# The second column group of the first batch's keys, formed by one whole unit behind the first scores

## The chip, the cores and the metric

The kernel runs on one core of a Trainium2 chip. The metric is the device time of one execution in microseconds. Every time below comes from the runs of the kernel before the change, or from one profiled execution of it. In the profile the engines are called PE (TensorE matmul), PEld (TensorE weight load), DVE (VectorE), ACT (ScalarE), POOL (GpSimd) and SP (the engine that only issues transfers). A name such as L410 is line 410 of the kernel before.

## The reference, cut to what matters

The reference is one block of a Perceiver: a cross-attention of 128 query rows to 2048 context rows for each of 8 batches, then a causal self-attention, then a feed-forward layer with quantised numbers. Only the cross-attention's beginning is touched.

```python
q = (layernorm(x) @ Wq)          # x: 8 batches x 128 rows x 512
k = context @ Wk                 # context: 8 x 2048 x 384
v = context @ Wv
sim = einsum('bihd,bjhd->bhij', q, k) * SCALE     # 8 heads of 64
out = softmax(sim) @ v
x = x + out @ Wo + bo
# then x = x + self_attention(layernorm(x)), and x = x + feed_forward(layernorm(x))
```

All is computed in 32-bit floating point. TensorE runs such a product as two matmul instructions, so the profile shows two MATMUL rows for each product of the program.

## The kernel before, in words

**Keys and values.** The context is handed over transposed, with 384 rows (three blocks of 128) and 2048 columns. A batch has two halves of 1024 columns, `x_{b}_0` and `x_{b}_1`. The projections to keys and to values are cut into 4 x 3 x 2 blocks, and the usual 24 block products are replaced by 20 (`block_product`), which need sums of blocks: 20 additions over a half of the context (`sum_half`, L168) and 13 additions with 4 copies over the weights (`sum_w`, copies at L185, additions L189 to L202). A key unit (`k_proj`, L410) makes one of two column groups `f2` of the keys; its `halves` say for which context halves. With both halves it has 40 matmul calls with 256 columns, with one half 20. A value unit (`v_proj`, L433) makes the values of one half. The units write seven PSUM banks, which are read as soon as they are whole: by ScalarE copies (L329) and by VectorE additions (L332 and L335, one operand in PSUM; L367, both operands in SBUF). A later product into the same bank waits for that reading.

**The start.** The first half of the first batch's keys is made without sums, by `k_plain` (L392, copies at L399): for each column group 12 matmul calls with 512 columns. Beside them the queries are prepared in two groups of four batches. `q_norm` computes each row's statistics on VectorE (L454, L456), the root on ScalarE (L457) and the normed rows on VectorE (L458, L460). `q_turn` transposes them on TensorE (L94) with ScalarE copies (L95), and `q_proj` projects them (L477, copies L481) and stores the result to DRAM (L482), from where `load_q` brings each batch's part.

**The order around the change.** TensorE, ScalarE and VectorE keep the order in which the program is written. Before the change it is: weight sums for keys (VectorE), plain keys of group 0, norm of the first four rows, plain keys of group 1 up to a point in its second half, transposes of the first rows, norm of the last four rows, the rest of the plain keys, projections with the second transposes between them. Meanwhile VectorE forms the sums of both context halves and of the value weights, and then prepares the self-attention's weights: `dot` and `weight_by_bias` (L268), which multiply a weight by a row of biases, and `turn_weight` (L281), which transposes a weight in 32 x 32 blocks that are then moved by 16 transfers on SP (L285). On GpSimd, `bo` is loaded into a buffer that the first L268 row must have left (L847), and added to the eight query tiles (L486). Then come the key unit of group 0 for the second half only, the values of the first half (with the second L268 row and the second L281 row in its VectorE order), the first scores (L509, evacuated at L513), the key unit of group 1 for the second half only with the first exponentials (L533), the product of two self-attention weights (`both_weights`, L296), and the values of the second half. From there on the loop is regular. `next_half(b, h)` loads a context half of a later batch on SP (L129) and forms its sums on GpSimd (L168); it can begin once the half that had the buffer has been read for the last time. The strips of the turned probabilities (L552) are on SP too.

**The loads at the start.** The key weights come in six transfers on ScalarE's queue (L214), the first context half in six on SP (L222), then four query tiles (L232), the query weights, the last four query tiles (L235), the second context half, the value weights and the self-attention weights.

Of the kernel before, what the change touches and what calls it, by code (L numbers as in the profile page):

```python
# [9 lines left out]
F32 = mybir.dt.float32  # L10
# [10 lines left out]
P = 128  # L21
# [4 lines left out]
def tile_perceiver_block(  # L26
# [21 lines left out]
    nc = tc.nc  # L48
    B, S, D = x.shape
# [15 lines left out]
    GB = B // NG  # L65
# [22 lines left out]
    xs = {}  # L88
# [17 lines left out]
    pp, ptp, tmp, xp = right("pp", 1), right("ptp", 1), right("tmp", TMPB), right("xp", 2)  # L106
# [15 lines left out]
    def x_tiles(b, h):  # L122
        xraw[b, h] = ctxp.tile([P, NKC, 4, BK], F32, tag=f"x{h}", name=f"x_{b}_{h}")
        xmore[b, h] = ctxp.tile([P, 8, BK], F32, tag=f"m{h}", name=f"m_{b}_{h}")
# [84 lines left out]

    w_in = keep.tile([P, 2, NKC, D], F32, tag="keep", name="w_in")  # L210
    wk, wv = w_in[:, 0], w_in[:, 1]
    for f2 in range(2):
        for k in range(NKC):
            nc.scalar.dma_start(wk[:, k, ts(f2, 256)], xa_wk[ts(k, P), ts(f2, 256)])  # L214

    early = bank("early")
    for _ in range(EARLY):
        nc.tensor.matmul(early[:, :P], ident, ident, start=True, stop=True)
    x_tiles(0, 0)
    for n in range(2):  # L220
        for k in range(NKC):
            nc.sync.dma_start(  # L222
                xraw[0, 0][:, k, 2 * n : 2 * n + 2],
                ctx_t[0, ts(k, P), ts(n, 512)].rearrange("p (i j) -> p i j", i=2),
            )

    x_in = ptp.tile([P, B, D], F32, tag="pT", name="x_in")
    for b in range(B):
        xs[b] = x_in[:, b, :]
    xd = dram.tile([P, B, D], F32, tag="xd", name="xd")  # L230
    for b in range(GB):
        nc.sync.dma_start(xs[b], x[b])  # L232
    wq = load_w(wop, xa_wq, NK, "wq", nc.sync)
    for b in range(GB, B):
        nc.sync.dma_start(xs[b], x[b])  # L235
    load_half(0, 1)
# [69 lines left out]
    wv3 = wv.rearrange("p k (j n) -> p k j n", j=2)  # L306
    wk_sums = wxa.tile([P, len(WSLOT), 2, P], F32, tag="wk_sums", name="wk_sums")
    wv_sums = wxa.tile([P, len(WSLOT), 256], F32, tag="wv_sums", name="wv_sums")
    sum_w(lambda k, j: wk4[:, k, :, j, :], wk_sums, nc.vector)

    kts, vts, ps_, sums, qts, turned_, pos, nms, wides, mxs = [
        {} for _ in range(10)
    ]
# [70 lines left out]
    def k_plain(f2):  # L384


        k_tile(0, f2)
        for n in range(2):
            pss = [bank(f"k_{f2}_{j}_{n}") for j in range(2)]
            for k in range(NKC):  # L390
                for j in range(2):
                    nc.tensor.matmul(  # L392
                        pss[j], wk4[:, k, f2, j, :], xraw[0, 0][:, k, 2 * n : 2 * n + 2],
                        start=(k == 0), stop=(k == NKC - 1),
                    )
                if (n, k) == (1, 0):
                    yield
            for j in range(2):
                nc.scalar.copy(kts[0, f2][:, j, ts(n, 512)], pss[j])  # L399

# [390 lines left out]
    def all_of(unit):  # L791
        for _ in unit:
            pass

    def first_of(unit):
        next(unit)
        return unit

    def next_half(b, h):
        if b < B:  # L800
            load_half(b, h)
            sum_half(b, h, nc.gpsimd)
# [19 lines left out]
        sa0.bv, sa0.u, sa0.mask = w[2:]  # L822
        return sap, w, sa0

    all_of(k_plain(0))
    both = [q_norm(0)]
    rest = first_of(k_plain(1))
    qds = [q_turn(0, both[0])]
    both.append(q_norm(1))
    all_of(rest)  # L830
    q_proj(0, both[0], qds[0], range(2))
    qds.append(q_turn(1, both[1]))

# [21 lines left out]
    first_of(values)  # L855
    turn_weight(1)
    all_of(values)
    next_half(1, 0)

    wo = load_w(wop, xa_wo, NK, "wo", nc.sync, tag="wq")  # L860

# [35 lines left out]
    for b in range(B):  # L897
        last = b + 1 == B
        for m in range(NK):
            scores(b, m)  # L900

            if m % 2 and not last:
                after_strips(b, m)
            if m == 1 and b > 0 and not last:
                load_u(b - 1)
            if m == 3 and b > 0 and not last:
                nc.scalar.dma_start(xtd[:, :, ts(b - 1, S)], stats[b - 1])
                nc.scalar.dma_start(xr[:, b - 1, :], xs[b - 1])
            if m == 3 and b < B - 2:
                load_x(b)  # L910
            unit = None
            if m > 0:
                attend(b, m - 1)
            elif b > 0:

                attend(b - 1, NK - 1)
            if m == 0:
                unit = v_proj(b, 1)
            elif not last and m == 1:
                unit = v_proj(b + 1, 0)  # L920
            elif not last:
                unit = k_proj(b + 1, m - 2)
            elif m == 1:
                unit = sa0.keys(sa0.rows)
            elif m == 2:
                unit = sa0.weights_and_values(sa0.rows[:3])
            else:

                sa1 = SelfAttention(1, sap, w)
            if b == m == 0:  # L930

                keys = k_proj(0, 1, (1,))
                first_of(keys)
                first_of(keys)
                exps(b, m, 0)
                all_of(keys)
            else:
                exps(b, m, 0)
                if unit and not (last and m > 0):
                    first_of(unit)  # L940
            if m == 3 and last:
                bring_rows()
                for r in sa0.rows:
                    sa0.probabilities(r)
# [24 lines left out]
            if unit:  # L969
                all_of(unit)  # L970
            if m == 1 and b > 0 and not last:
                row_scale(b - 1)
            if m == 3:
                next_half(b + 2, 0)
            if m == 0:
                next_half(b + 1, 1)
                if not last:
                    load_q(b + 1)
                if b > 0:
                    project(b - 1, ot)  # L980
                if last:
                    sap, w, sa0 = enter_self_attention()
# [189 lines left out]
    for i, unit in enumerate(work):  # L1172
# [7 lines left out]
        if i > 2:  # L1180

            b = i - 3
# [63 lines left out]
```

## Time and profile before

| what | us |
|---|---|
| median of 3 runs (lowest, highest) | 1086.6 (1086.08, 1086.62) |
| the profiled execution's own time | 1086.99 |
| its span on the core | 1085.2 |
| TensorE busy with matmuls | 1079.3 |
| VectorE busy | 757.9 |
| ScalarE busy | 352.4 |
| GpSimd busy | 234.3 |

The stages at the beginning, in the chain of work that ended last (start in us): plain keys from 4.9, first transposes at 23.5, the remaining plain keys at 25.3, query projections at 28.7, half-unit of the keys at 57.9, values at 67.2, first scores at 84.4, product of weights at 98.3, values of the second half at 112.0, second scores at 129.3.

To read the lines that follow: a row of the timeline gives start, duration, engine, line, operation, what is written and read, and in brackets how long the engine had been idle and what ended that. A row of stretches gives for each engine its busy time in the stretch, then the clock granted to TensorE (1.00 is full), the busy share of the DMA engines and their rate. "Landing" is the time from the issue of a transfer to its last byte.

### The profile page before, as it was taken

Reading aid. Unit: us, or ns where it says so; the run is one execution under the profiler, and the core shown is the slowest. Engines: PE = TensorE matmul, PEld = TensorE weight load, DVE = VectorE, ACT = ScalarE, POOL = GpSimd, SP = SyncE. Lnnn points to the kernel's source line nnn. Section 1 sums busy time; section 2 is a strip of 40 time slices with the busy share of each in tenths; the row PEclk is TensorE's granted clock in tenths of the full one; section 3 lists DMA queues with packets and bytes.
Section 4 is the critical chain, followed back from the end, with each engine's and each line's share of the span. In section 5 each row is a group of like instructions: output and inputs, shape, how many; then the busy total and the mean of one; then the engine's idle time right before and its main releaser. Section 6 shows DMA issues by size and latency. Waiting matters only on the chain.

```text
span 1085.2 us, 16609 instructions
## 1 busy us (share of the span) xinstructions
PE 1079.3 (99%) x6198; PEld 816.0 (75%) x6198; DVE 757.9 (70%) x1639; ACT 352.4 (32%) x559; POOL 234.3 (22%) x350
## 2 busy tenths in 40 slices
PE   9999999999999999999999999999999999999998
PEld 5475788878887888787777878887888656768875
DVE  4876567778777877787778777777877657584233
ACT  3322233324332423432343234332433222323221
POOL 0144040351045005500550054025100212000000
PEclk9999999999999999999999999999999999999999
DMA  9476334553565456545544653555345644431001
GB/s 326 139 186 152 118 80 98 136 146 84 131 156 134 95 131 156 136 89 132 147 120 98 157 146 78 118 137 146 79 109 149 197 129 146 175 104 32 10 12 57
DMA packets 71855, 134.81 MB, mean 124 GB/s; under 512 B 28240, under 2 KB 36448, under 8 KB 70752
## 3 DMA queue, kind: packets, MB, share of 16 engines
q1 hardware_dynamic: 61120, 113.03, 40.7%
q0 software_dynamic: 3312, 11.03, 3.2%
q10 hardware_dynamic: 7344, 9.70, 2.9%
q8 instruction: 49, 0.80, 0.3%
q14 instruction: 30, 0.25, 0.1%
HBM read 54.01 MB, written 10.49 MB: 59 GB/s over the span
## 4 chain that ended last, share of the span: by engine, by line
PE 97%; SPq 1%; DMA 1%; DVE 1%; ACT 0%; issue 0%
PE pv_z L433 21%; PE pk_z L410 20%; PE po L564 11%; PE sc L509 10%; PE pv_b L433 4%; PE pk_b L410 3%; PE ph_b L1071 3%; PE psk L720 3%; PE psv L764 3%; PE pf L1119 3%; PE pq L477 3%; PE py L647 3%; PE ph_c L1071 2%; PE ph_a L1071 2%; PE k L392 2%; PE ph L1023 1%
## 5 line engine op out<-in xcount | busy, mean ns | idle before, releaser
L533 ACT ACTIVATE p<-p,nm 128x2048 f32<-128x2048 f32 x64 | 128.2, 2003 | 274.9 <-DVE nm L521 158.8
L546 DVE STREAM_TRANSPOSE p<-p 128x512 f32<-128x512 f32 x256 | 158.9, 679 | 63.1 <-ACT p L533 62.9
L513 DVE TENSOR_SCALAR_CACHE_REDUCE p<-sc 128x512 f32<-128x512 f32 x256 | 159.0, 686 | 20.9 <-PE sc L509 20.9
L168 POOL TENSOR_TENSOR m<-x 128x256 f32<-128x256 f32 x70 | 51.2, 732 | 495.5 <-DMA x<-in_ctx_t_dram 421.0
L433 PE MATMUL pv_z<-wv_sums,x 128*128 128x256 f32 x640 | 157.9, 381 | 0.0
L410 PE MATMUL pk_z<-x,wk_sums 128*128 128x256 f32 x600 | 150.0, 382 | 0.7 <-ACT kt L329 0.6
L433 PEld LDWEIGHTS pv_z<-wv_sums,x 128*128 128x128 f32 x640 | 120.6, 190 | 18.5 <-issue 2.2
L564 PEld LDWEIGHTS po<-pT,v 128*64 128x64 f32 x2048 | 111.1, 137 | 23.8 <-issue 22.3
L410 PEld LDWEIGHTS pk_z<-x,wk_sums 128*128 128x128 f32 x600 | 112.5, 190 | 20.3 <-issue 2.0
L564 PE MATMUL po<-pT,v 128*64 128x128 f32 x2048 | 118.9, 274 | 0.0
L509 PE MATMUL sc<-kt,q 64*128 64x512 f32 x512 | 118.5, 602 | 0.0
L433 PE MATMUL pv_z<-wv_sums,m 128*128 128x256 f32 x448 | 107.4, 380 | 0.0
L410 PE MATMUL pk_z<-m,wk_sums 128*128 128x256 f32 x420 | 101.4, 380 | 0.0
L433 PEld LDWEIGHTS pv_z<-wv_sums,m 128*128 128x128 f32 x448 | 83.4, 190 | 12.6 <-issue 0.8
L509 PEld LDWEIGHTS sc<-kt,q 64*128 64x128 f32 x512 | 46.9, 186 | 59.5 <-issue 54.6
L410 PEld LDWEIGHTS pk_z<-m,wk_sums 128*128 128x128 f32 x420 | 78.4, 190 | 11.7 <-DVE kt L332 0.4
L329 ACT COPY v<-pv_z 128x512 f32<-128x512 f32 x112 | 62.8, 589 | 55.8 <-PE pv_z L433 55.5
L329 ACT COPY kt<-pk_z 128x512 f32<-128x512 f32 (+1 forms) x112 | 59.8, 562 | 58.7 <-PE pk_z L410 58.2
L168 POOL TENSOR_TENSOR x<-x 128x256 f32<-128x256 f32 x98 | 69.9, 732 | 0.6 <-DMA x<-in_ctx_t_dram 0.6
L332 DVE TENSOR_TENSOR v<-pv_z,v 128x512 f32<-128x512 f32 x96 | 63.1, 685 | 5.5 <-PE pv_z L433 5.5
L332 DVE TENSOR_TENSOR kt<-pk_z,kt 128x512 f32<-128x512 f32 (+1 forms) x96 | 60.0, 651 | 5.9 <-PE pk_z L410 5.6
L332 DVE TENSOR_TENSOR v<-pv_b,v 128x512 f32<-128x512 f32 x48 | 32.9, 686 | 40.4 <-PE pv_b L433 40.4
(208 smaller groups left out, 1252.5 us busy)
## 6 DMA issues: line engine op xcount, KB each, us to landing
pT<-p SPq DMA_DIRECT2D x488, 128.0 KB, 2.3
x<-in_ctx_t_dram SPq DMA_DIRECT2D x45, 512.0 KB, 5.6
w<-in_w_t_dram SPq DMA_DIRECT2D x1, 4096.0 KB, 12.7
w2f<-in_w_t_dram SPq DMA_DIRECT2D x16, 256.0 KB, 2.7
pT<-p POOLq DMA_DIRECT2D x24, 128.0 KB, 3.7
x_in<-in_x_dram SPq DMA_DIRECT2D x8, 256.0 KB, 7.1
qd<-xq SPq DMA_DIRECT2D x8, 256.0 KB, 2.5
q<-qd SPq DMA_DIRECT2D x8, 256.0 KB, 4.2
```

What stands on the lines that cost most here:

```text
L168: eng.tensor_tensor(x_block(b, h, to), x_block(b, h, one), x_block(b, h, two), ALU.add if op == "+" else ALU.subtract,)
L329: nc.scalar.copy(outs[ij], views(ps))
L332: nc.vector.tensor_tensor(outs[to], views(ps), outs[other], op)
L410: nc.tensor.matmul(ps[:, ts(i, BK)], wk_sums[:, WSLOT[WAT[r]], f2, :], x_block(b, h, XAT[r]), start=start and i == 0, stop=True, skip_grou ...
L433: nc.tensor.matmul(ps[:, ts(t, 256)], x[:, ts(t, P)], wv_sums[:, WSLOT[WAT[r]], :], start=start and t == 0, stop=True, skip_group_check=True,)
L477: nc.tensor.matmul(ps, wq[:, k, ts(m, P)], xt[:, k, :], start=(k == 0), stop=(k == NK - 1),)
L509: nc.tensor.matmul(pair[i], q[r, :], kts[b, m // 2][r, m % 2, ts(n, 512)], start=True, stop=True)
L513: nc.vector.tensor_scalar(p[:, :, i].rearrange("p g (t i) -> p t g i", i=SQ)[:, ts(n, Q)], pair[i].rearrange("p (t g i) -> p t g i", g=Q, ...
L533: nc.scalar.activation(p[:, :, i], p[:, :, i], AF.Exp, bias=nms[b, m][:, i : i + 1], scale=SCALE, accum_out=sums[b][:, h : h + 1],)
L546: nc.vector.transpose(p[:, g, i], p[:, g, i])
L564: nc.tensor.matmul(pos[b][h * DH : (h + 1) * DH, ts(m, P)].rearrange("p (a i) -> p a i", a=Q), v[:, jt % 8, ts(2 * m + h, DH)], turned_[b, ...
L1071: nc.tensor.matmul(self.ps[to][:, ts(t, HR)], w[:, q, 2 * self.d + t], x[:, q], start=start and t == q == 0, stop=True, skip_group_check=True,
```

## The change

The second column group of the first batch's keys is no longer made by `k_plain` for the first half and by a half-unit for the second; one unit with both halves behind the first scores makes all of it. So `next_half(1, 0)` moves behind that unit, since the unit still reads the first half. The second half of the key weights goes from ScalarE's queue to SP, behind the query weights. The first four query tiles are loaded between the two column halves of the context, and `q_norm(0)` is written ahead of the plain keys. The key weights' sums go behind both norms.

```diff
-    for f2 in range(2):
+    def load_keys_half(f2, eng):
         for k in range(NKC):
-            nc.scalar.dma_start(wk[:, k, ts(f2, 256)], xa_wk[ts(k, P), ts(f2, 256)])
+            eng.dma_start(wk[:, k, ts(f2, 256)], xa_wk[ts(k, P), ts(f2, 256)])
+
+    load_keys_half(0, nc.scalar)
...
     for n in range(2):
         for k in range(NKC):
             nc.sync.dma_start(
                 xraw[0, 0][:, k, 2 * n : 2 * n + 2],
                 ctx_t[0, ts(k, P), ts(n, 512)].rearrange("p (i j) -> p i j", i=2),
             )
...
-    for b in range(GB):
-        nc.sync.dma_start(xs[b], x[b])
+        for b in range(2 * n, 2 * n + 2):
+            nc.sync.dma_start(xs[b], x[b])
     wq = load_w(wop, xa_wq, NK, "wq", nc.sync)
+    load_keys_half(1, nc.sync)
     for b in range(GB, B):
         nc.sync.dma_start(xs[b], x[b])
...
-    sum_w(lambda k, j: wk4[:, k, :, j, :], wk_sums, nc.vector)
...
-                if (n, k) == (1, 0):
-                    yield
...
-    all_of(k_plain(0))
     both = [q_norm(0)]
-    rest = first_of(k_plain(1))
+    k_plain(0)
     qds = [q_turn(0, both[0])]
     both.append(q_norm(1))
-    all_of(rest)
+    sum_w(lambda k, j: wk4[:, k, :, j, :], wk_sums, nc.vector)
     q_proj(0, both[0], qds[0], range(2))
     qds.append(q_turn(1, both[1]))
...
     all_of(values)
-    next_half(1, 0)
...
-                keys = k_proj(0, 1, (1,))
+                keys = k_proj(0, 1)
                 first_of(keys)
                 first_of(keys)
                 exps(b, m, 0)
                 all_of(keys)
+                next_half(1, 0)
```

More of the change, by code (lines that the diff above doesn't have):

```diff
@@ L219, in tile_perceiver_block @@
     x_tiles(0, 0)
+    x_in = ptp.tile([P, B, D], F32, tag="pT", name="x_in")
+    for b in range(B):
+        xs[b] = x_in[:, b, :]
+    xd = dram.tile([P, B, D], F32, tag="xd", name="xd")
     for n in range(2):
@@ L225, in tile_perceiver_block @@
             )
[L227 to L230, printed above, removed]
-    for b in range(GB):
-        nc.sync.dma_start(xs[b], x[b])
+        for b in range(2 * n, 2 * n + 2):
+            nc.sync.dma_start(xs[b], x[b])
     wq = load_w(wop, xa_wq, NK, "wq", nc.sync)
+    load_keys_half(1, nc.sync)
     for b in range(GB, B):
```

## The prediction

> **What bounds the kernel now.** I read the page's engine shares first, then the chain of work that ended last for the opening 100 us, since the whole edit lies there.
>
> ```profile
> PE 1079.3 (99%) x6198; PEld 816.0 (75%) x6198; DVE 757.9 (70%) x1639; ACT 352.4 (32%) x559; POOL 234.3 (22%) x350
> ...
> PE 97%; SPq 1%; DMA 1%; DVE 1%; ACT 0%; issue 0%
> ```
>
> TensorE is busy for 99% of the span, so on paper each matmul saved is time saved. But a busy share over the whole span says nothing of a stage where another engine could become the limit, so the stages come next (stretch; busy us of PE, PEld, DVE, ACT, POOL; granted clock; DMA share; GB/s):
>
> ```profile
> 4.90:28.70 23.80, 23.80 (x65) 11.60 (x66) 14.81 (x41) 10.52 (x19) 0.00 (x0) 1.00 1.02 367
> 28.70:57.90 29.20, 29.20 (x81) 13.86 (x81) 25.75 (x69) 9.35 (x18) 5.92 (x11) 1.00 0.38 125
> 57.90:67.20 9.30, 9.18 (x41) 7.46 (x41) 4.77 (x12) 3.19 (x8) 8.32 (x8) 1.00 0.63 173
> ...
> 84.40:98.10 13.70, 13.14 (x58) 8.92 (x58) 10.41 (x31) 6.38 (x11) 1.64 (x3) 1.00 0.72 169
> ...
> 161.29:178.75 17.46, 17.46 (x82) 15.09 (x82) 12.51 (x20) 7.16 (x11) 0.00 (x0) 1.00 0.56 122
> ```
>
> The rows are: plain keys with the first transposes; query projections; the half-unit of the first keys; first scores with the half-unit of the second keys; and, for size, a later full key unit. In the second row VectorE works 25.75 of 29.2 us: it is almost as full as TensorE. Its own order of time shows where it stands when the keys' half-unit begins (start, duration, group, idle time before it):
>
> ```profile
> 54.70 2.48 DVE L281 STREAM_TRANSPOSE w_sa<-w_sa 128x512 f32<-128x512 f32 x4
> 60.50 0.42 DVE L335 TENSOR_TENSOR kt<-kt,pk_z 128x256 f32<-128x256 f32 x1 [3.31 <-ACT kt L329]
> ...
> 64.57 0.76 DVE L367 TENSOR_TENSOR kt<-kt 128x256 f32<-128x256 f32 x1
> ...
> 67.56 2.29 DVE L268 SCALAR_TENSOR_TENSOR unread<-w_sa,row 128x512 f32<-128x512 f32 x1
> ```
>
> VectorE is free at 57.2 and TensorE asks at 57.9, so before the change the slack of VectorE against TensorE is only 3.3 us.
>
> **What the change does, part by part.** *Matmuls.* The plain second column group is 24 of the 48 L392 matmuls (two per fp32 product). They start every 0.43 us, so 10.3 us leave the stretch before the query projections. The half-unit after the first scores becomes a whole one. From the rows above, scores plus half-unit take 13.7 us; scores (3.63 in the chain) plus a whole unit take 3.63 + 17.46 = 21.1. That is 7.4 us given back. If nothing else moved, TensorE would gain 10.3 - 7.4 = 2.9 us: 1.7 of arithmetic (10.3 + 8.6 - 17.2), the rest from waits that double-length products hide (the half-unit stretch holds 8.6 us of matmuls in 10.1).
>
> *Query rows.* The first four rows now have 0.39 MB less ahead of them (the second half of the key weights), about 1.0 us at the 400 GB/s of that stretch. They land at 14.4 rather than 15.4 (last issue 8.5, 6.9 to landing). Statistics of the last row 0.77, aggregation 0.36, table load and root and reciprocal 1.9 and the first row's 0.54 give a normed row at 18.0. The plain keys end at about 16.4, so TensorE waits 1.6 us there. ScalarE now has the root ahead of the four key copies (L399): they run 17.2 to 19.3, then the four transposes' copies (L95, 2.05) until 21.4. Nothing stands between these transposes and the projection any more, so it starts at 21.5 against 28.68. Of the 10.3 us, 7.2 are left as lead.
>
> *The weight sums.* L189 to L202 go from idle time of VectorE (10.0 to 15.15) to behind both norms. This is the part that decides. The last four rows have the same bytes ahead of them as before:
>
> ```profile
> L235 SPq DMA_DIRECT2D x_in<-in_x_dram x4: 328/328/1203, 9.7 to 13.4; - x4
> ...
> DMA to landing us min/median/max: 7.4/7.4/9.1
> ```
>
> So the last lands at about 13.4 + 7.4 = 20.8, also afterwards. VectorE then: its statistics until 21.9, aggregation 22.3, root and reciprocal 0.63 (no table load this time) 22.9, norms 1.91 to 24.8, weight sums 5.2 to 30.0. L168 of the second half started at 28.29 before. From there to the end of the first L268 row (54.84) VectorE has 26.55 us, of which 1.78 was a wait for ScalarE's copies at L185; these come earlier now, since TensorE is ahead. 30.0 + 24.8 = 54.8. **VectorE reaches that point no earlier than before**, although TensorE is 7.2 us earlier.
>
> *TensorE waits for it.* The half-unit would start at 50.7 and be at its eleventh product (the one that reuses bank z1) 4.5 us later, at 55.2. That product waits for L335, queued behind four L281 transposes, at 57.2 to 57.6. Then comes L367, which reads two SBUF tiles. GpSimd's additions at L486 start when `bo` has landed, and `bo` waits for the same L268 row, so they keep their time, 58.9:
>
> ```profile
> 58.87 6.18 POOL L486 TENSOR_TENSOR x_in<-x_in,bo 128x512 f32<-128x512 f32 x5 [3.19 <-DMA bo<-in_xa_bo_dram]
> 64.99 0.55 POOL L487 DMA_DIRECT2D xd<-x_in  x1
> 65.56 3.72 POOL L486 TENSOR_TENSOR x_in<-x_in,bo 128x512 f32<-128x512 f32 x3
> ```
>
> Before, L367 (64.57) met only the tail of the fifth addition and took 0.76 instead of the 0.42 of its next call. Now it would be due at about 60.2, inside the run of five. Here the **Trainium skill** weighs against the change: "GPSIMD Engine Reference", section Key points, says that GpSimd shares its SBUF interfaces with VectorE, with contention where a VectorE instruction has two SBUF inputs. It doesn't say how long one waits. The nearest row is L268 at 67.56: 2.29 us instead of 0.70, ending 0.56 after the last of the additions and not after the one that was running. By that row L367 is held until the gap at 65.05 and ends at 65.3, as before; then 1.85 us (as before: 65.33 to 67.18) to the first values. If it got in at the next boundary between two additions (each 1.24) it would end about 3.7 us earlier. I take the L268 row, the same kind of instruction against the same GpSimd group; the other end is kept as a rival.
>
> *Sum.* Values start at 67.2 as before; with them, turning of the weights and first scores at 84.4 as before; then +7.4 us for the whole unit. The lead is eaten and the debt is paid: +7.4 us on the profiled execution (1087.0, span 1085.2), and on the median 1086.6 that makes **1094.0**.
>
> *What hides and costs nothing.* The second half of the key weights moves to SP, 0.39 MB ahead of the last four rows; the sums need it only at about 24. Three more SP issues of about 0.35 us wait behind earlier landings anyway; the context half behind them landed at about 24.7 and is needed at 30. `next_half(1, 0)` (three loads, then 20 GpSimd operations L168, 15 us) now waits for the whole unit's last read and stands on SP ahead of the strips of the first scores. The strips wait for VectorE's transposes (L546), which still start as the unit ends, 3.7 us ahead of the first strip; three issues take 1.5. The sums are ready some 20 us after the unit and `v_proj(1, 0)` comes 38 us after it (98.1 to 136.5), GpSimd's next half 35 us. Without that cover the loss would be the sums' 15 us in part; I see none. The bound is 0 to 1 us.
>
> *A wait with a price of its own.* TensorE would stand for about 5 us in front of L367. The skill's "TensorE: Matmul & The Clock Gate", section Part 1, says that after an idle window of some 3.4 us the clock halves, and comes back after a busy window. No stretch of this trace shows such an idle time: the granted clock is 1.00 in all rows above. By the row the cost is 0; by the rule, an estimate of up to one window at half rate with the next only partly counted, 1.7 to 3.4 us. I take 0, as 5 us need not hold a whole aligned window, and keep 3.4 as the upper end.
>
> *Loads that come sooner.* DMA moved 205 GB/s at 8 to 10 us and 281 at 10 to 12, against 400 later: 3.4 us of transfer lost. If the new order avoids that, the last row lands at 17.4, ScalarE's copies become the limit, the weight sums end near 27.2, and the total is +4.6. If it adds to it, +1.
>
> **Rivals.** (a) *GpSimd lets L367 in* at the next boundary: +3.7 with landings as before, +0.9 with the early ones. For it: the two-element L521 got through at such boundaries (0.60 at 209.79). Against: L268. About 1090.3. (b) *Not slower: L367 isn't held at all*, because `bo` lands 1.3 us late (it now meets the load of `wo`, issued at about 51) and the additions begin behind L367. Place: the end of the half-unit, which then runs straight on from L335 and ends near 62.3, so 62.3 - 67.2 + 7.4 = +2.5; each microsecond by which the last query row lands before 20.8 comes off. It decides from 20.5 on: below that it is within 0.2% (about 2.2 us, what a measurement of this kernel can tell from no change). Against: the four L268 behind would then meet the additions. About 1087.8. (c) *Faster*: TensorE waits neither for rows nor for VectorE, 1086.6 - 2.9 = 1083.7. The lead of 7.2 alone only pays for the 7.4, so this also needs the wait of 3.1 us around the first transposes to go. (d) *Worse*: the clock halves and the four L268 of the second row meet the additions, so that turning the second weight delays the values' banks: +11 or more, 1098.
>
> **How the numbers follow.** Main case 0.62, with its own range 1091.2 (loads early) to 1097.4 (clock halves); (a) 0.20, three quarters of it above 0.2%; (b) 0.09; (c) 0.04; (d) 0.05. Slower: 0.62 + 0.15 + 0.05 = 0.82; same: 0.09 + 0.05 = 0.14; faster 0.04. The range 1088.3 to 1097.8 leaves out (b), (c), a little of (a), and (d): about 0.2.
>
> **What would show it.** L94's first transpose near 18.0 and L477's first matmul near 21.5. L189 of the key weights near 24.8, L168 near 30, L281 near 54.7 as before. Idle TensorE of 7 us in all within L410's first unit, waiting on L335 and then on VectorE behind L367, and L367 itself at several us instead of 0.76. L433 near 67.2, first scores (L509) near 84.4, the products at L296 near 105.5 instead of 98.1. The prediction is wrong if the last query row lands far from 20.8, if L367 takes under 1.5 us though GpSimd adds beside it, or if L433 starts before 63.

## The result, and the profile after

| what | before | after |
|---|---|---|
| median of 4 runs (lowest, highest), us | 1086.52 (1086.08, 1086.62) | 1091.20 (1090.90, 1091.38) |
| ratio, 95% interval | | 1.0044, 1.0031 to 1.0057 |
| the profiled execution's own time, its span, us | 1086.99, 1085.2 | 1091.15, 1089.2 |

The changed kernel is slower by 4.7 us. In the changed kernel a line number differs by a few: L393 are the plain keys, L476 the query projections, L409 the key units, L432 the values, L271 the rows of the self-attention's weights (before: L268), L284 their turning (L281), L336 and L333 the additions that read a PSUM bank (L335, L332), L368 the one that reads SBUF alone (L367), L485 GpSimd's additions (L486), L845 the load of `bo`.

The engines' shares and the shares of the chain that ended last, from the page of the changed kernel:

```profile
PE 1079.7 (99%) x6214; PEld 818.8 (75%) x6214; DVE 765.2 (70%) x1639; ACT 350.3 (32%) x554; POOL 235.5 (22%) x350
...
PE 92%; DVE 5%; DMA 2%; issue 0%; ACT 0%; DVEq 0%; ACTq 0%
```

TensorE is as busy as before, but 5% of the chain now runs through VectorE and 2% through transfers (1% each before). The chain in order of time shows where (start, duration, work):

```profile
5.32 12.69 PE k L393 x24
...
21.47 1.46 DVE xq L459 x3
...
52.68 2.35 DVE w_sa L284 x4
...
65.02 4.22 DVE unread L271 x2
```

From 21.5 to 55 us the path is VectorE's alone, and again from 61 to 74. The same stages as a table of stretches (busy us of PE, PEld, DVE, ACT, POOL; granted clock; DMA share; GB/s):

```profile
4.90:9.60 4.70, 4.28 (x5) 1.85 (x6) 1.34 (x2) 0.00 (x0) 0.00 (x0) 1.00 1.05 375
9.60:17.83 8.23, 8.23 (x21) 3.56 (x19) 4.18 (x12) 3.12 (x5) 0.00 (x0) 1.00 1.05 383
...
20.62:49.94 29.32, 29.32 (x80) 13.97 (x81) 27.98 (x76) 10.11 (x22) 5.39 (x10) 1.00 0.60 212
49.94:60.35 10.41, 9.43 (x42) 7.35 (x40) 9.26 (x24) 3.19 (x8) 3.78 (x4) 1.00 0.61 176
60.35:79.84 19.49, 17.89 (x82) 14.85 (x80) 18.87 (x27) 4.10 (x7) 10.86 (x12) 1.00 0.79 180
...
83.47:101.01 17.54, 17.54 (x83) 15.47 (x82) 10.66 (x24) 8.09 (x11) 0.00 (x0) 1.00 0.06 9
```

They are: the plain keys' slow beginning and the rest of them, the query projections, the half-unit, the values, and the whole key unit behind the first scores. VectorE works 28.0 of 29.3 us beside the projections (25.75 of 29.2 before) and 18.9 of 19.5 beside the values.

In the kernel before, TensorE started the half-unit, the values, the first scores and the product behind the key unit at these times (last line: that product with the change):

```profile
57.74 1.03 PE L410 MATMUL pk_z<-x,wk_sums 128*128 128x256 f32 x4
...
67.02 1.89 PE L433 MATMUL pv_z<-wv_sums,x 128*128 128x256 f32 x8
...
84.38 3.71 PE L509 MATMUL sc<-kt,q 64*128 64x512 f32 x16
...
98.09 13.90 PE L296 MATMUL pw<-turned_w 128*128 128x512 f32 x32
```

```profile
100.84 9.60 PE L299 MATMUL pw<-turned_w 128*128 128x512 f32 x22
```

With the change TensorE starts the half-unit 7.8 us sooner (49.94), the values 6.7 sooner (60.35) and the first scores 4.5 sooner (79.84). So 1.1 us of the lead go in the half-unit and 2.1 in the values. It leaves the whole key unit 2.8 late, is 3.2 behind at 522 us and at 983, and 4.0 behind at the end.

Where the lead goes is seen in what TensorE waits for (its rows with idle time between the projections and the scores):

```profile
20.62 7.13 PE L476 MATMUL pq<-xq,wq 128*128 128x512 f32 x16 [0.89 <-ACT xq L95]
55.38 0.70 PE L409 MATMUL pk_z<-x,wk_sums 128*128 128x256 f32 x2 [0.96 <-DVE kt L336]
70.09 1.13 PE L432 MATMUL pv_z<-wv_sums,x 128*128 128x256 f32 x4 [0.95 <-DVE v L336]
74.46 1.13 PE L432 MATMUL pv_z<-wv_sums,m 128*128 128x256 f32 x4 [0.65 <-DVE v L333]
```

and in VectorE's and then GpSimd's order of time there:

```profile
54.95 0.38 DVE L336 TENSOR_TENSOR kt<-kt,pk_z 128x256 f32<-128x256 f32 x1
...
58.00 0.66 DVE L368 TENSOR_TENSOR kt<-kt 128x256 f32<-128x256 f32 x1
...
60.89 0.69 DVE L271 SCALAR_TENSOR_TENSOR unread<-w_sa,row 128x512 f32<-128x512 f32 x1
...
61.67 1.58 DVE L271 SCALAR_TENSOR_TENSOR unread<-w_sa,row 128x512 f32<-128x512 f32 x1
...
63.34 1.58 DVE L271 SCALAR_TENSOR_TENSOR unread<-w_sa,row 128x512 f32<-128x512 f32 x1
...
65.02 4.15 DVE L271 SCALAR_TENSOR_TENSOR unread<-w_sa,row 128x512 f32<-128x512 f32 x1
...
69.39 0.65 DVE L336 TENSOR_TENSOR v<-v,pv_z 128x512 f32<-128x512 f32 x1
...
57.11 7.26 POOL L485 TENSOR_TENSOR x_in<-x_in,bo 128x512 f32<-128x512 f32 x5 [3.60 <-DMA bo<-in_xa_bo_dram]
...
64.88 3.72 POOL L485 TENSOR_TENSOR x_in<-x_in,bo 128x512 f32<-128x512 f32 x3
```

GpSimd's additions start at 57.1. L368 gets through in 0.66. But three of the four L271 rows behind it take 1.58, 1.58 and 4.15 us instead of 0.70: together 5.2 us too long. L336 of the values, queued behind them, comes at 69.39, and TensorE waits for it.

The last four query rows, as the `x_in` tile's rows of the changed kernel show them (issues and landing):

```profile
L238 SPq DMA_DIRECT2D x_in<-in_x_dram x4: 327/328/455, 10.2 to 12.6; - x4
...
DMA to landing us min/median/max: 4.9/6.3/7.0
```

In the trace each has its own landing: the last was issued at 12.56 and landed at 19.30. Before, it was issued at 13.37 and landed at 20.80.

### The profile page after: what moved, and what is told of

Read it like the earlier page. It is cut to its first block, busy times and chain, and to the rows that moved or that the text cites. A ratio compares the mean times of both kernels' runs of the same rounds, so it can differ in the third digit from the quotient of the medians.

```text
span 1089.2 us, 16636 instructions
## 1 busy us (share of the span) xinstructions
PE 1079.7 (99%) x6214; PEld 818.8 (75%) x6214; DVE 765.2 (70%) x1639; ACT 350.3 (32%) x554; POOL 235.5 (22%) x350
## 4 chain that ended last, share of the span: by engine, by line
PE 92%; DVE 5%; DMA 2%; issue 0%; ACT 0%; DVEq 0%; ACTq 0%
PE pv_z L432 21%; PE pk_z L409 21%; PE po L563 11%; PE sc L508 11%; PE pv_b L432 4%; PE pk_b L409 4%; PE ph_b L1069 3%; PE psk L719 3%; PE psv L763 3%; PE pf L1117 3%; PE py L646 3%; PE ph_c L1069 2%; PE ph_a L1069 2%; DMA w2f<-in_w_t_dram 2%; PE pw L299 1%; PE k L393 1%
## 5 line engine op out<-in xcount | busy, mean ns | idle before, releaser
L168 POOL TENSOR_TENSOR m<-x 128x256 f32<-128x256 f32 x70 | 51.3, 733 | 501.8 <-DMA x<-in_ctx_t_dram 338.4
L432 PE MATMUL pv_z<-wv_sums,x 128*128 128x256 f32 x640 | 158.0, 381 | 0.9 <-DVE v L336 0.9
L409 PE MATMUL pk_z<-x,wk_sums 128*128 128x256 f32 x620 | 153.9, 382 | 1.0 <-DVE kt L336 1.0
L432 PEld LDWEIGHTS pv_z<-wv_sums,x 128*128 128x128 f32 x640 | 120.4, 190 | 19.9 <-issue 2.4
L409 PEld LDWEIGHTS pk_z<-x,wk_sums 128*128 128x128 f32 x620 | 116.4, 190 | 20.5 <-issue 2.0
L432 PE MATMUL pv_z<-wv_sums,m 128*128 128x256 f32 x448 | 107.7, 380 | 0.6 <-DVE v L333 0.6
L409 PE MATMUL pk_z<-m,wk_sums 128*128 128x256 f32 x434 | 104.4, 379 | 0.0
L432 PEld LDWEIGHTS pv_z<-wv_sums,m 128*128 128x128 f32 x448 | 83.3, 190 | 13.9 <-DVE v L333 1.0
L409 PEld LDWEIGHTS pk_z<-m,wk_sums 128*128 128x128 f32 x434 | 81.0, 190 | 12.2 <-DVE kt L333 0.4
L330 ACT COPY kt<-pk_z 128x512 f32<-128x512 f32 (+1 forms) x112 | 61.5, 576 | 62.9 <-PE pk_z L409 62.7
L168 POOL TENSOR_TENSOR x<-x 128x256 f32<-128x256 f32 x98 | 70.2, 736 | 0.4 <-DMA x<-in_ctx_t_dram 0.4
L333 DVE TENSOR_TENSOR v<-pv_z,v 128x512 f32<-128x512 f32 x96 | 63.1, 684 | 5.5 <-PE pv_z L432 5.5
L333 DVE TENSOR_TENSOR kt<-pk_z,kt 128x512 f32<-128x512 f32 (+1 forms) x96 | 61.6, 668 | 5.3 <-PE pk_z L409 5.2
L333 DVE TENSOR_TENSOR v<-pv_b,v 128x512 f32<-128x512 f32 x48 | 32.9, 686 | 39.0 <-PE pv_b L432 38.8
```

Source lines behind the costliest of these rows:

```text
L168: eng.tensor_tensor(x_block(b, h, to), x_block(b, h, one), x_block(b, h, two), ALU.add if op == "+" else ALU.subtract,)
L330: nc.scalar.copy(outs[ij], views(ps))
L333: nc.vector.tensor_tensor(outs[to], views(ps), outs[other], op)
L409: nc.tensor.matmul(ps[:, ts(i, BK)], wk_sums[:, WSLOT[WAT[r]], f2, :], x_block(b, h, XAT[r]), start=start and i == 0, stop=True, skip_grou ...
L432: nc.tensor.matmul(ps[:, ts(t, 256)], x[:, ts(t, P)], wv_sums[:, WSLOT[WAT[r]], :], start=start and t == 0, stop=True, skip_group_check=True,)
```

## The experiments

Every experiment was timed beside the kernel before on the same chip; its ratio to that kernel is the number to compare. The medians of the kernel before were 1086.81 for the first four experiments, 1086.86 for the next three and 1086.68 for the last three.

### GpSimd's additions put behind the values

```diff
-    bo = tmp.tile([P, D], F32, tag="t", name="bo")
-    nc.gpsimd.dma_start(bo, xa_bo.partition_broadcast(P))
-    for g in range(NG):
-        keep_rows(g)
     turn_weight(0)
...
     all_of(values)
+    bo = tmp.tile([P, D], F32, tag="t", name="bo")
+    nc.gpsimd.tensor_copy(bo[:, :1], vts[0, 0][:, 0, 1, D - 1 :])   # waits for the last value
+    nc.gpsimd.dma_start(bo, xa_bo.partition_broadcast(P))
+    for g in range(NG):
+        keep_rows(g)
```

> The changed kernel with the load of bo and GpSimd's eight additions held back until the first values are whole. Theory (VectorE sets the time, and its weight-by-bias rows of two SBUF inputs are held by GpSimd's additions): the four rows take 0.70 us each instead of 0.69, 1.58, 1.58 and 4.15, the two waits of TensorE within the first values (together 2.2 us) go, and the kernel takes about 1089.0 us, 2.2 less than the changed one; the first values take 17.2 us. Rival (the waits come from VectorE's own amount of work there, with GpSimd only beside it): no gain, 1091.

Measured: median 1090.13 (1088.21 to 1092.01), ratio 1.0028, interval 1.0018 to 1.0039. The median lies between the two theories, and the runs spread widely. The two lowest, 1088.21 and 1088.26, have a mean clock of 1.000, and the one at 1088.38 has 0.999; of the other five, four have 0.997 to 0.999 and lie between 1089.97 and 1092.01, and the fifth, 1090.28, has 1.000. The profiled execution, 1091.26, is one of the four. VectorE's order in it:

```profile
60.17 0.43 DVE L368 TENSOR_TENSOR kt<-kt 128x256 f32<-128x256 f32 x1
...
65.19 0.70 DVE L271 SCALAR_TENSOR_TENSOR unread<-w_sa,row 128x512 f32<-128x512 f32 x1
...
67.41 0.69 DVE L336 TENSOR_TENSOR v<-v,pv_z 128x512 f32<-128x512 f32 x1 [1.22 <-ACT v L330]
```

No row is held any more and L336 of the values waits for nothing of VectorE's. So the additions are what stretched the L271 rows, and the values take 17.4 us again (62.28 to 79.64), as before the change: the 2.1 us lost there were theirs. But TensorE's wait in the half-unit is longer now, because in this execution TensorE came 0.8 us sooner and VectorE's L336 0.6 later, and a stretch at half clock follows it; the wait, and the stretches:

```profile
55.99 1.22 PE L409 MATMUL pk_z<-x,wk_sums 128*128 128x256 f32 x2 [2.34 <-DVE kt L336]
```

```profile
49.17:56.02 6.85, 4.51 (x22) 3.64 (x20) 6.53 (x17) 2.83 (x7) 0.00 (x0) 1.00 0.68 196
56.02:59.44 3.42, 3.42 (x8) 2.79 (x9) 1.41 (x4) 0.37 (x1) 0.00 (x0) 0.50 0.44 62
```

Two things remain of the loss: the wait for L336 (behind the turning L284), and the half clock behind it. The two lowest runs are 3.0 below the changed kernel's median, but the medians differ by 1.1 only and the two intervals overlap. The half clock explains a part of the spread, not all of it: the run at 1090.28 had none of that length.

### The key weights' sums left out

```diff
-    sum_w(lambda k, j: wk4[:, k, :, j, :], wk_sums, nc.vector)
+    for w in WSLOT:
+        if isinstance(w, tuple):
+            nc.scalar.copy(wk_sums[:, WSLOT[w]], wk4[:, w[0], :, w[1], :])
```

The tile is cleared once instead, so the 13 additions L189 to L202 (5.2 us of VectorE) aren't computed and the keys that the units make aren't those of the reference.

> The changed kernel without the 13 additions of the key weights' sums (left out; the tile is cleared instead and only the four copies are made, so the keys of the sums are wrong). Theory (VectorE's amount of work between the last query row and the half-unit sets the time): VectorE is 5.2 us earlier at the weight-by-bias rows, L336 of the half-unit is ready before TensorE gets to its eleventh product, the additions end before most of the second four rows, and all but a little of the 3.2 us of waits goes: about 1087.3. Rival (the waits come from TensorE's own lead and the unit's seven banks): 1091 as before.

Measured: median 1089.41 (1088.18 to 1089.85), ratio 1.0023, interval 1.0013 to 1.0032. VectorE is now early for the half-unit (L336, here L337, comes at 53.32 after 1.5 us of idle time). Against the kernel before beside it, 2.1 us are won; the 1087.3 of the theory is missed by as much. `bo` waits for an L271 row of VectorE's, so it is loaded 3.2 us sooner too (issued at 49.75 for 52.97), and GpSimd's additions move along (54.72 for 57.11). Now L368 (here L369) takes 1.34, and one L271 row again 4.15:

```profile
57.38 1.34 DVE L369 TENSOR_TENSOR kt<-kt 128x256 f32<-128x256 f32 x1
...
61.73 4.15 DVE L271 SCALAR_TENSOR_TENSOR unread<-w_sa,row 128x512 f32<-128x512 f32 x1
```

A faster VectorE brings the collision forward with it. Of the 3.3 us that TensorE loses in the half-unit and the values with the change, 0.9 are left here; a further 0.9 go at 984 us, for a reason that the last three experiments show.

### The keys' part alone, on the kernel before

```diff
-    rest = first_of(k_plain(1))
...
-    all_of(rest)
...
-    next_half(1, 0)
...
-                keys = k_proj(0, 1, (1,))
+                keys = k_proj(0, 1)
...
+                next_half(1, 0)
```

> The kernel before with the key part alone: plain keys of group 1 and the half-unit replaced by one whole unit behind the first scores; loads, norms and weight sums where they were. Theory (VectorE sets the time): TensorE's projections start at about 23.1, 2.5 us later than in the changed kernel, but the half-unit ends at about the same time, so the result is near the changed kernel's, 1090.5 to 1091.5. Rival (TensorE's lead at the projections sets it): 2.5 us more than the changed kernel, 1093.7. Other rival (moving the weight sums behind the norms is what costs): near 1087.

Measured: median 1094.04 (1092.31 to 1094.65), ratio 1.0063, interval 1.005 to 1.0075, near the 1093.7 of the first rival. Each of its runs is above each run of the whole change. TensorE's first transposes, and the clock in the stretches around them:

```profile
20.45 3.67 PE L94 MATMUL pt_q<-ident,xq 128*128 128x128 f32 x16 [4.54 <-DVE xq L460]
```

```profile
4.90:18.20 13.30, 10.81 (x24) 4.37 (x24) 7.65 (x21) 4.94 (x10) 0.00 (x0) 1.00 1.02 347
18.20:28.44 10.24, 7.32 (x21) 4.86 (x22) 8.19 (x22) 3.92 (x7) 0.00 (x0) 0.50 1.04 395
```

The plain keys of the second group were the cover under which the query rows landed and were normed. Without them TensorE stands for 4.5 us, runs 10.24 us at half clock, and reaches the half-unit only 1.8 us sooner than before. Most of the lead is lost at once and the debt of 7.4 us stays. The new order of loads and norms is what lets the change keep a lead at all.

### The order alone, with the keys as before

The edit against the kernel before:

```diff
+    load_keys_half(0, nc.scalar)                 # and the second half on SP behind wq
...
-    for b in range(GB):
-        nc.sync.dma_start(xs[b], x[b])
+        for b in range(2 * n, 2 * n + 2):
+            nc.sync.dma_start(xs[b], x[b])
...
-    all_of(k_plain(0))
     both = [q_norm(0)]
+    all_of(k_plain(0))
     rest = first_of(k_plain(1))
...
+    sum_w(lambda k, j: wk4[:, k, :, j, :], wk_sums, nc.vector)   # moved from the top
```

> The changed kernel with the keys as before (plain keys of group 1, half-unit behind the first scores, next half in its old place), so only the order of loads, norms and weight sums is changed. Theory: TensorE isn't early any more, VectorE is ready when asked, and what is left is the plain keys' later start and later context columns, about 1 us: 1087.7. Rival (the new order itself costs the time): 1090 or more.

Measured: median 1090.70 (1090.39 to 1090.96), ratio 1.0036, interval 1.0022 to 1.0049. The 1087.7 that my theory gave is missed by 3 us. VectorE's order shows why:

```profile
26.07 0.18 DVE L459 RECIPROCAL qrs<-qsd 128x4 f32<-128x4 f32 x1 [5.52 <-ACT qsd L458]
...
30.07 0.42 DVE L189 TENSOR_TENSOR wk_sums<-w_in,wk_sums 128x256 f32<-128x256 f32 x1 [1.87 <-ACT wk_sums L185]
...
72.80 4.16 DVE L271 SCALAR_TENSOR_TENSOR unread<-w_sa,row 128x512 f32<-128x512 f32 x1
```

The root of the second norm (L458) is queued on ScalarE behind copies that wait for TensorE, so VectorE stands for 5.5 us, and its weight sums start 7.2 us later than with the whole change (22.84); the rest is as in the changed kernel, the L271 rows under GpSimd's additions included. So either half of the change costs time by itself, and by different means. The two losses don't add: together they cost 4.7 us, alone 7.2 and 3.9.

### The loads put back

```diff
+    load_keys_half(1, nc.scalar)
...
-        for b in range(2 * n, 2 * n + 2):
-            nc.sync.dma_start(xs[b], x[b])
+    for b in range(GB):
+        nc.sync.dma_start(xs[b], x[b])
     wq = load_w(wop, xa_wq, NK, "wq", nc.sync)
-    load_keys_half(1, nc.sync)
```

> The changed kernel with the order of loads of the kernel before: both halves of the key weights on ScalarE's queue, the four query tiles behind the whole first context half. Theory (the earlier landing is worth something): the last query row lands at 20.8 again instead of 19.3, the first normed row comes at about 18 or later, so VectorE is 1.5 us later throughout and TensorE waits for it in the half-unit; about 1092.7, 1.5 above the changed kernel, and up to 3.4 more if the longer wait costs a window of clock. The prediction's own sum, which took this landing, gives 1094.0. Rival (landings don't matter, since VectorE's reserve covers them): 1091.2 as with the change.

Measured: median 1092.07 (1091.21 to 1094.47), ratio 1.0056, interval 1.0042 to 1.007. It lies between the two theories, and its interval overlaps the changed kernel's, so the median doesn't decide. The last row landed at 20.61, 1.3 us later than with the change and as the theory had it, and VectorE's weight sums began 2.2 us later (25.08). But in the profiled execution (1091.21) that cost nothing by the first scores, 79.96 for 79.84: TensorE waited 2.67 us for the first rows and ran 6.8 us at half clock (0.996 mean), so it came to the half-unit 3.7 us later and found L336 done; and `bo` landed later, so that the L271 rows took 0.88, 1.58, 1.58, 1.58. The landing is late, but other waits cover it.

### The additions late, and the first turning behind the half-unit

To the first experiment's edit is added:

```diff
-    turn_weight(0)
     all_of(k_proj(0, 0, (1,)))
+    turn_weight(0)
     weight_by_bias(1)
```

> The changed kernel with GpSimd's additions behind the values, as in the late-additions run, and the first turned weight's four transposes on VectorE (2.5 us) moved behind the half-unit of the keys. Theory: the eleventh product's bank is then read in time, no wait of 1 to 1.5 us stands in the half-unit and no window of half clock follows; values start about 1.2 us sooner than in the late-additions run, at about 57 to 59; total 1086.5 to 1087.5, about what the kernel before has, because a lead of 8 us and a debt of 7.4 us cancel. Rival (the transposes delay the values' banks instead, or the strips of the turned weight come late for the product of weights): no gain on the late-additions run, 1088.2 to 1090.

Measured: median 1086.75 (1086.32 to 1087.51), ratio 1.0000, interval 0.9992 to 1.0008; the mean clock is 1.0 in all 13 runs. TensorE's rows at the eleventh product, at the values and at the scores carry no wait:

```profile
52.98 0.70 PE L409 MATMUL pk_z<-x,wk_sums 128*128 128x256 f32 x2
...
57.71 1.89 PE L432 MATMUL pv_z<-wv_sums,x 128*128 128x256 f32 x8
...
75.07 3.70 PE L508 MATMUL sc<-kt,q 64*128 64x512 f32 x16
```

The values start at 57.7, within the expected 57 to 59, and the scores 9.3 us sooner than before the change. The key unit ends 2.0 us sooner than before (96.07 for 98.09); up to 0.8 of this may be the start, where the full clock came earlier in this execution than in that of the kernel before. The two delays on VectorE, turning and additions, together therefore account for the change's loss as far as it can be measured. The turning was not moved alone, so how the loss divides between the two is not shown.

### The additions late on the kernel before

The first experiment's edit, made on the kernel before.

> The kernel before with the same late load and additions on GpSimd alone. Theory (before the change the additions met nothing on the path: one row of 2.29 us in slack of VectorE): no difference, 1086.6, within 0.5 us; the values start at 67.2 as before. Rival (the late additions are worth something by themselves, so the gain of the late-additions run is not owed to the change): 1085.5 or less.

Measured: median 1086.88, ratio 1.0000, interval 0.9992 to 1.0008. The L268 row that took 2.29 us before takes 0.70 and it gains nothing: there it was in VectorE's slack. The collision was present before the change; the change moved it onto the path.

### Fewer TensorE instructions at the start

In the profile of the kernel with the late turning, the 2.0 us won by 98 us are down to 0.45 at 984. VectorE's last cast of `w2f` waits for its load, additions stand behind it, and TensorE waits 1.2 us for one of them. That load takes 4.7 us there; in the kernel before it takes 2.7. The changed kernel loses 0.8 us at the same place. The DMA queues during the last `w2f` load, first of the changed kernel (982.7 to 987), then of the kernel before (979.2 to 982.1):

```profile
q1 hardware_dynamic: 243, 0.43, 36.4%
q8 instruction: 1, 0.02, 2.3%
issues: line engine op xcount, KB each, median us to landing
w2f<-in_w_t_dram SPq DMA_DIRECT2D x1, 256.0 KB, 4.1
```

```profile
q1 hardware_dynamic: 248, 0.44, 50.4%
issues: line engine op xcount, KB each, median us to landing
w2f<-in_w_t_dram SPq DMA_DIRECT2D x1, 256.0 KB, 2.7
```

In the changed kernel one instruction packet of 16 KB falls into the load; before, that packet came at 985.0, behind the landing at 982.0. Queue 8 has 49 such packets for the 12428 matmuls and weight loads of TensorE, one for about 254. The Trainium skill ("Runtime: NRT & Kernel Launch", section Instruction fetch mechanics) says that an engine fetches its instructions in blocks of 16 KiB, 256 instructions, and that this is mostly hidden. The merged keys add 32 TensorE instructions, so the block's end comes sooner in the program. In all six traces in which the packet falls into that load, TensorE loses 0.5 to 1.7 us there against the kernel before; in those in which it doesn't, nothing. The edit takes instructions away at the very start, on this kernel and two others:

```diff
-    for _ in range(EARLY):                       # 7
-        nc.tensor.matmul(early[:, :P], ident, ident, start=True, stop=True)
+    wide = wk_sums[:, :2].rearrange("p a b n -> p (a b n)")[:, : EARLY * P // 2]
+    nc.vector.memset(wide, 0.0)
+    for _ in range(2):
+        nc.tensor.matmul(early[:, : EARLY * P // 2], ident, wide, start=True, stop=True)
```

On the kernel with late additions and late turning:

> The run with the turned weight later, and the seven small products at the very start (28 TensorE instructions) replaced by two of the same summed length on a cleared tile (8 instructions). Nothing else moves but TensorE's count of instructions, 20 fewer. In the traces one 16 KB instruction packet falls into the flight of the last w2f load in every kernel with the merged keys that loses time at 983 to 988 (load 3.7 to 4.7 us), and after it in those that don't (2.6 us). Theory: the packet comes some 2.2 us later (16 instructions in 1.73 us there), behind the landing; the last w2f load takes 2.7 instead of 4.7, TensorE's wait of 1.2 us before the last turned rows goes, total about 1085.3, 1.4 below the same kernel without this. Rival (the load is slow for another reason): 1086.7 as without it; or a later full clock at the start, then 1 to 3 us more.

Measured: median 1085.87 (1085.20 to 1086.99), ratio 0.9992, interval 0.9984 to 1.0. The last `w2f` load takes 2.6 us and lands at 982.08; the packet now comes at 982.33, and TensorE's wait before the last turned rows is gone. The gain is 0.9 us by the two medians, 0.7 if each is compared with the kernel before that was timed beside it, where 1.4 were expected; the two intervals overlap. The best version found is thus 0.8 us below the kernel before, which is within 0.2%, so the two can't be told apart.

On the changed kernel:

> The changed kernel with the same two products at the start in place of seven. Theory: the packet at 983.8 goes to about 986.0, behind the landing at 985.4; the 0.8 us that the changed kernel loses there go, about 1090.4. Rival: 1091.2 as with the change.

Measured: median 1090.46 (1090.15 to 1091.91), ratio 1.0035, interval 1.0022 to 1.0049. The last `w2f` load takes 2.75 instead of 4.13, and what is lost around 985 us (0.8) is lost no longer. Each against its own kernel before, the medians differ by 0.9, as expected (0.7 as they stand), but the intervals overlap; only the profile shows the effect. The profiled execution, 1091.91, is the slowest of the five. At its half-unit TensorE comes 0.8 us sooner than in the changed kernel (49.16 for 49.94) and VectorE's L338 1.7 later, mostly because VectorE stood 1.2 us for a row of biases to land. VectorE's wait, TensorE's, and the stretch at half clock, which begins within TensorE's wait:

```profile
50.44 0.70 DVE L274 SCALAR_TENSOR_TENSOR unread<-row,row 128x512 f32<-128x512 f32 x1 [1.22 <-DMA row<-line]
```

```profile
57.07 1.22 PE L411 MATMUL pk_z<-x,wk_sums 128*128 128x256 f32 x2 [3.43 <-DVE kt L338]
```

```profile
55.71:62.54 6.83, 5.47 (x13) 4.39 (x14) 4.43 (x10) 0.37 (x1) 4.06 (x4) 0.50 0.48 104
```

On the kernel before:

> The kernel before with the same two products at the start. Theory: the packet lies behind the last load already, so nothing changes, 1086.6 within 0.5. Rival (the start itself is better or worse so): any other time.

Measured: median 1086.45, ratio 0.9998, interval 0.999 to 1.0007: no change, as expected.

## Why the prediction was right, and which of its steps were not

"Slower", with a chance of 0.82, came true. The likeliest time, 1094.0, was 2.8 us too high, inside the range of 1088.3 to 1097.8. The debt held, and VectorE does eat a part of the lead; but it eats less of it than was foreseen, and at another place. TensorE's times against the kernel before, by stage (us):

| | predicted | profile |
|---|---|---|
| lead at the start of the half-unit | 7.2 | 7.8 |
| lost in the half-unit | 7.2 | 1.1 |
| lost in the values | 0 | 2.1 |
| lost in the whole key unit | 7.4 | 7.3 |
| lost later (0.4 by 320 us, 0.8 to 0.9 at 984) | 0 | 1.3 |
| behind at the end | 7.4 | 4.0 |

The steps that were foreseen, with their measured sizes, sum to 0.6 us behind (1.1 + 7.3 - 7.8), less than the 2.2 us that the prediction takes as the least that can be told from no change. The other 3.4 come from terms that the sum put at nothing. That the time lies inside the range is luck to that extent. Two of the signs that the prediction named for its being wrong came true: L367 took under 1.5 us while GpSimd added beside it (0.66), and the values started before 63 (60.35).

**The debt of 7.4: right.** From the first scores to the product behind the whole unit it took 100.84 - 79.84 = 21.0, against the 21.1 of the sum and 13.7 before.

**The lead at the projections: 7.2 predicted, 7.9 measured** (20.62 for 28.52). The rows were not the limit here: the fourth landed at 12.6, not at 14.4, and the first was normed at 16.0, not at 18.0. TensorE was late instead: its plain keys ended at 18.0, not 16.4, because they began 0.4 later and the first five matmuls took 4.28 us, 0.86 each, where the others took 0.43; in the kernel before only the first three were slow. So the first transposes stand at 17.83, close to the 18.0 that was foreseen, for another reason: that is luck.

**"So the last lands at about 13.4 + 7.4 = 20.8, also afterwards": wrong by 1.5.** The bytes ahead were the same but the last row was issued 0.8 sooner and landed in 6.7. The rate did not fall to 205 and 281 GB/s as it did before: in the same two stretches of 2 us it was 348 and 389. The side case "loads that come sooner" named this, but its sum is wrong: 205 and 281 against 400 are 1.6 us lost, not 3.4. With 1.6 it gives 19.2, and 19.30 was measured. VectorE's steps after it follow: L189 22.84 for 24.8, L168 28.01 for 30.0, the first rows' end 52.7 for 54.8. So "VectorE reaches that point no earlier than before" failed by 2.1 us, of which 1.5 are the landing.

**L335 in front of the eleventh product: right in kind.** Asked at about 54.4, done at 55.3, TensorE waits 0.96 where about 2 were foreseen.

**"L367 is held until the gap at 65.05": wrong, and this is the step of the sum that failed.** It met the run of five additions, as foreseen, but took 0.66 and not some 5. Of the two rows weighed for it, the cheap one (a two-element addition that got through at a boundary) was the right one. With that the values start at 60.35, not 67.2.

**What took its place: the four rows behind it.** They were written down only as what speaks against rival (b), and as half of rival (d) at +11 or more. They cost 5.2 us of VectorE. Of that, 2.1 us reach TensorE: values to scores took 19.5 us where they took 17.4 before, and 17.4 with the additions late. The contention that the prediction cited from the Trainium skill ("GPSIMD Engine Reference", section Key points), with VectorE instructions that have two SBUF inputs, pointed at the right pair. Which of them gets in soon is what the prediction couldn't read, and the traces don't explain it either: a row that started 0.69 us into an addition got in at its end (61.67), and one that started 0.77 into one, in the kernel before, did not (67.56).

**The clock at 0: right for this kernel, too easy in general.** Two of its four executions have a mean clock of 1.0 and two of 0.998, and they take the same time. But waits of 2.3 to 4.5 us go with a half clock in four of the experiments' profiles. In the first experiment TensorE was busy for all of the 3.42 us at half clock, which is 1.7 us of work lost; so the prediction's estimate of 1.7 to 3.4 us, from the Trainium skill ("TensorE: Matmul & The Clock Gate", section Part 1), was of the right size. The mean clock of a run does not tell its time by itself: with the loads put back, the two fastest runs (1091.2) have 0.996 and the two slowest (1094.0 and 1094.5) 0.998.

**Costed at nothing, and not nothing: the count of instructions.** Nothing in the prediction looked at 983 us. The 32 instructions more put one fetch of TensorE's code into a load that VectorE and then TensorE wait for: 0.8 us in the profile.

**The bill.** By the medians: 1091.2 with the change; 1090.1 with the additions late (1088.2 in its two fastest runs); 1086.75 with the turning late as well; 1085.9 with the fetch out of the way. Additions and turning together bring it to the kernel before; the single steps of 1.1 and 0.9 have overlapping intervals. Rival (c), 2.9 us faster, was what the arithmetic of TensorE allows; 0.8 is what all the repairs together reached. What remains between them wasn't sought.

## What to carry to other kernels

When an edit gives the bound engine a lead, ask which engine is then last and what stands in its order in front of the work that the lead needs: here transposes that could wait stood ahead of the additions that free a PSUM bank, and so did row products that GpSimd slowed. An engine's instructions that share memory access with another's come into collision at new places when either is moved, and speeding up the one that triggers the other carries the collision along. Work that looks like waste can be the cover of a landing: the plain keys that were removed hid the query rows.

## What the hardware showed that was not expected

- **VectorE under GpSimd's additions.** A row product with two SBUF inputs, 0.70 us alone, took 1.58 where it got in at the end of the addition that was running (started at 61.67, that addition ended at 62.7), and 4.15 when it was let in only after the group's end (started at 65.02, past two ends of additions at 66.1 and 67.3). GpSimd suffers too: its five additions took 7.26 us instead of 6.18; the two at whose start a row product got in took 1.72 each instead of 1.27. VectorE's additions with one operand in PSUM took 0.37 to 0.43 us in the same stretch, no more than elsewhere. Why one row got in and the next did not stays open.
- **A wait shorter than a window halves the clock.** Of the 3.41 us ahead of the half clock in the first experiment, TensorE stood idle for 2.34 and was working for the rest; in the three other profiles with a half clock, 2.1 to 2.5 of these 3.41 us were idle. The half clock came in whole multiples of 3.41: one after 2.34 us of idle time, two after 2.67 (the loads put back) and after 3.43 (the changed kernel with fewer instructions), three after 4.54 (the keys alone). Waits of up to 1.23 us (the late turning, at 983) left the clock at 1.00. Other executions of the first experiment's kernel have a mean clock of 1.000; whether their wait was shorter isn't known, as one execution of each is profiled. The Trainium skill ("TensorE: Matmul & The Clock Gate", section Part 1) speaks of at least one idle window of about 3.4 us; a wholly idle one was not needed here.
- **The clock at the start isn't in the row.** The first stretch of the changed kernel is shown at a granted clock of 1.00, but its matmuls take 0.86 us against 0.43 later. How long that lasts differs by execution: the 24 plain matmuls took 12.69 us in the changed kernel's profile and 10.57 in the first experiment's. A difference of a microsecond between two single profiles can be this alone.
- **Instruction packets are transfers.** A 16 KB packet of TensorE's queue took 1.55 us at 983.8 in the changed kernel, and the 256 KB load around it 4.13 instead of 2.7.
